# A decoder layer on one core: layernorm of the cross units' tokens moved to where the tokens are made, their rows kept normalized in HBM, and the light parts placed anew

## The chip, the core and the metric

The kernel runs on one core of one Trainium2 chip. The core has five engines with a queue of instructions each: TensorE (PE in the profile; its weight loads are PEld) for matmuls, VectorE (DVE), ScalarE (ACT), GpSimd (POOL), and SyncE (SP), which here only issues DMAs. Each engine works through its queue in order and waits on semaphores for the others. The time is the device time of one execution in microseconds; the figure compared is the median of several executions.

## The reference

Four sequences of 1024 tokens with 512 features, in float32, go through three blocks, each added to its input:

```python
x = x + attn(layernorm(x))            # 16 heads of 32, queries, keys and values from x
x = x + xattn(layernorm(x), ctx_768)  # queries from x, keys and values from a context of 384 features
x = x + ffn(layernorm(x))             # 512 -> 64; 16 relu units for each of the 64; 64 -> 512
```

`layernorm` subtracts the mean over the 512 features and divides by the square root of the variance plus 1e-5. The first attention is gated: the softmax of the scores is multiplied by an aperture for each query and an expression for each key (two sigmoids of `x @ Wa` and `x @ We`) and normalized again; its output is rotated for each head and projected. The second attention is a plain one with biases.

## The kernel before

The work is cut into eight **units**, `order = [(ph, b)]`: units 0 to 3 are the first attention (`ph` 0) of the four sequences, units 4 to 7 the cross attention (`ph` 1) and the feed-forward network. A unit has two **halves** (`hf`) of 512 query tokens. A half's `attention(u, hf)` has 32 **steps**: four groups of four heads (`g`), eight blocks of 128 keys each (`kt`). A step issues the scores (L552), two exponentials on ScalarE (`e`, L557), sums of the exponentials on VectorE (`es`, L563 and L565; in `ph` 0 also the gated sum `eg`, L573), and then the previous step's values times exponentials (`av`, L579) and, in units 0 to 3 and 7 ("shared"), a part of the sums on TensorE (`sm`, L587). When a group is over, `normalize` copies `av`; one step later `add_up` has TensorE add up `es` over the partitions (L609), and the result goes through HBM (`sum_d`, `rec_d`) to `divide` two steps later and `multiply` (L659) two more.

Beside these steps run the **light parts** of other work: `pre(u)` makes a coming unit's inputs (load of tokens, layernorm, transposes, projections `k`, `q` and values `v`, gates), `post(u, hf)` finishes a half (output projection `o` L716, and in `ph` 1 layernorm, network, output). `beside(u, hf)` writes by hand the list of parts that go with a half, and `run` deals them out: each part has a load (2 for two chunks of a projection, 0 for what does no matmul), and after each step parts are issued until their share of the total load matches the share of steps. `weave` spreads the parts of one list evenly among those of another, `pause` is load without work. The queues of TensorE, VectorE, ScalarE and GpSimd have exactly this order; SP's order is made by a scheduler.

A transpose of tokens goes in two moves. `away` writes normalized rows to HBM (`rows_d`, L295) and `back` reads them into another layout with four DMAs (L300); then VectorE transposes blocks of 32 x 32 (`blocks`, L306: four instructions, `tr`). Only the very first tokens are transposed by TensorE (`across`, L313).

What the change touches:

- In `ph` 0, `post` writes the new tokens twice: `x1_d` as they are (L718), and `x1b_d` with the cross attention's output bias added by GpSimd (L720). In `ph` 1, `pre` loads `x1_d` again (L366), takes the statistics (`stats`, L378), their root (`root`, twelve small instructions), normalizes (`norm`, L286), writes the rows and reads them back.
- In `ph` 1, `post` does the same for the feed-forward network: statistics with each `o` (L726), `root` (L731), four `norm`, each into one of two buffers `r2` that a DMA writes to `rows_d`; the last of them also reads back into `xn`. Each `norm` is followed by an addition of `bout_bc` on GpSimd (L747). Then `tr`, `inputs` (L758, which reads `xn`), `hidden` (17 pieces, L773 on ScalarE and L779 on VectorE) and `outputs` (L790, L796).
- `rows_d` lies in three buffers that take turns. The tile `tok` (one buffer) holds both a unit's loaded tokens and `xn`; `inT` (two buffers) holds transposed tokens or context.
- In the prelude, before the first step, `negate` (L142) turns the sign of the gates' bias `nbae`, which eight small DMAs bring.
- While `crossing` is set, that is in all of the eight units, `evacuate` copies on ScalarE, else on VectorE.

Of the kernel before, what the change touches and what calls it, by code (L numbers as in the profile page):

```python
# [16 lines left out]
P = 128  # L17
# [46 lines left out]
def moderate_path(tc: tile.TileContext, a: dict, out: bass.AP, flag: bass.AP):  # L64
    nc = tc.nc
    x = a["x"]
    with ExitStack() as st:
# [26 lines left out]
        x1_d = [[dram.tile([P, D], F32, tag=f"mx1_{b}_{t}", name="x1_d") for t in range(NT)] for b in range(B)]  # L94
# [193 lines left out]
        turns = [0]  # L288

        def away(rows, xt, t, n):  # L290

            if t == 0:
                rows[:] = [dram.tile([4, P, D], F32, tag=f"rows_{turns[0] % 3}", name="rows_d")]
                turns[0] += 1
            nc.sync.dma_start(rows[0][t : t + n].rearrange("t p d -> p t d"), xt)  # L295

        def back(rows, to):

            for q in range(NC):
                nc.sync.dma_start(  # L300
                    to[ts(q, NB)].rearrange("j t (s f) -> j (t s) f", f=P),
                    rows[0].rearrange("t (s j) f -> j (t s) f", j=NB)[:, :, ts(q, P)],
                )
# [36 lines left out]
        def pre(u):  # L340
# [15 lines left out]
            def load_x(hf):  # L356
                def f():
                    if u == 0 and hf == 0:
                        xt = x0
                    else:  # L360
                        xt = p1.tile([P, 4, D], F32, tag="tok", name="xin")
                        if ph == 0:
                            nc.sync.dma_start(xt, x[b].rearrange("(t p) d -> p t d", p=P)[:, 4 * hf : 4 * hf + 4, :])
                        else:
                            for t in range(4):
                                nc.sync.dma_start(xt[:, t, :], x1_d[b][4 * hf + t])  # L366
                    me["xn", hf] = xt
                return f

            def ln(hf):  # L370
# [14 lines left out]
                def norm(t):  # L385
                    def f():
# [4 lines left out]
                        if t % 2:  # L391
                            away(res.setdefault("rows", []), me["xn", hf][:, t - 1 : t + 1, :], t - 1, 2)
                        if t == 3:
                            me["xT", hf] = p2.tile([P, 4, D], F32, tag="inT", name="xT")
                            back(res["rows"], me["xT", hf])
# [131 lines left out]
            for k, f, load in (  # L527
                ("ctx", load_ctx, 0), ("x", load_x, 0), ("g", gates, 1), ("gt", gates_t, 1),
# [154 lines left out]
        def post(u, hf):  # L683
# [18 lines left out]
            def project(t):  # L702
                def part(cs):
                    def f():
# [11 lines left out]
                        nc.vector.tensor_tensor(r, res["po"], r, ALU.add)  # L716
                        if ph == 0:
                            nc.sync.dma_start(x1_d[b][4 * hf + t], r)  # L718
# [3 lines left out]
                        else:  # L722
                            s6 = p2.tile([P, 6], F32, tag="bnst1", name="bnst1")
                            if t == 0:
                                res["mv"] = p2.tile([P, 4, 2], F32, tag="fmv", name="fmv")
                            nc.vector.bn_stats(s6, r)  # L726
                            nc.vector.bn_aggr(res["mv"][:, t, :], s6)
# [3 lines left out]
            def root():  # L731
                i = 2 * NS + b * NT + 4 * hf
                nc.gpsimd.tensor_copy(marks[:, i : i + 4], res["mv"][:, :, 1])
                res["rs"] = rsqrt(res["mv"], 4)
                res["xn"] = p1.tile([P, 4, D], F32, tag="tok", name="xn")

            def norm(t):
                def f():
                    if last:
                        normalized(res["xn"][:, t, :], res[t], res["mv"], res["rs"], t)  # L740
                    else:
                        r2 = p2.tile([P, 1, D], F32, tag="r2", name="r2")
                        normalized(r2[:, 0, :], res[t], res["mv"], res["rs"], t)
                        away(res.setdefault("rows", []), r2, t, 1)
                        if t == 3:
                            back(res["rows"], res["xn"])
                    nc.gpsimd.tensor_tensor(res[t], res[t], bout_bc, ALU.add)  # L747
                return [(0, f)]

# [3 lines left out]
            def inputs():  # L753
# [10 lines left out]
                nc.vector.tensor_copy(sT, ss[:, 0 : 2 * P])  # L764
# [37 lines left out]
            if ph == 0:  # L802
                return {"load": loads, "o": [project(t) for t in range(4)]}
            return {
                "load": loads,
                "o": [project(t) for t in range(4)],
                "ln": [[(0, root)]] + [norm(t) for t in range(4)],
                "tr": [[(1 if last else 0, tr(t))] for t in range(4)],
# [39 lines left out]
        def beside(u, hf):  # L848

            last = post(u, 0) if hf else post(u - 1, 1) if u else None  # L850
            if u + 1 == n:
                out = last["load"] + pause(16) + last["o"] + weave(last["ln"], pause(4)) + pause(4) + last["tr"]
                return out + pause(2) + last["s"] + weave(last["h"], pause(14)) + pause(2) + last["out"]
            p = pres[u + 1]
            x, ln, tr, k, q, v = (p[i] for i in ("x", "ln", "tr", "k", "q", "v"))
            next_ = pres[u + 2] if u + 2 < B else None
            if u + 1 < B:
                if hf == 0:
                    out = x[1] + k[0][0:1] + p["g"][0] + k[0][1:] + p["gt"][0]
                    if last:  # L860
                        out = last["load"] + out + weave(ln[1], last["o"])
# [3 lines left out]
                    return out + v[0][0:2] + tr[1] + v[0][2:3] + p["g"][1] + v[0][3:] + p["gt"][1]  # L865
                if not next_:
                    return k[1] + last["load"] + v[1] + last["o"] + q[0] + q[1]
                out = next_["x"][0] + k[1] + last["load"] + v[1] + last["o"] + weave(next_["ln"][0], q[0])
# [691 lines left out]
```

## Time and profile before

| | |
|---|---|
| median of three runs | 2329.31 us (2329.3 to 2330.63) |
| profiled execution | 2332.95 us, span 2331.2 us |
| mean granted clock of TensorE | 0.983 |
| TensorE busy | 2222.9 us, 95% of the span |
| VectorE, ScalarE, GpSimd busy | 1560.7, 1234.8, 142.5 us |
| HBM read and written | 124.07 and 51.15 MB |

The span is the time from the first to the last instruction of the profiled execution. The profile's slices are 40 equal parts of it, 58.3 us each, with busy tenths (9 is 90% or more); the row PEclk is the granted clock in tenths. A list of waits has the engine and line that waited, what ended the wait, microseconds in total, times, and the longest. A timeline line has the start, the time taken, engine, line, operation, the tile written and the tiles read, the number of instructions run together, and in brackets the idle time ahead and what ended it. The prelude ends and the first step begins at 119.5 us; second halves of units 4, 5 and 6 begin at 1350.3, 1616.0 and 1881.7 us, unit 7 at 2021.0 us.

### The profile page before, as it was taken

To read this page: it belongs to the slowest core of one execution; us is meant where nothing else is said; L and a number is where in the kernel's file an instruction comes from. 1 tells how busy PE (TensorE), PEld (TensorE's weight loads), DVE (VectorE), ACT (ScalarE), POOL (GpSimd) and SP (SyncE) were. 2 spreads that over 40 slices of the span, in tenths; PEclk is the share of its full clock that TensorE was granted. 3 is DMA by queue.
4 is the path that set the end of the run, shared out by engine and by line. 5 is a ranking of instruction groups with operands and counts; after the bars stand their busy time and mean duration, and the time that the engine had idled before them with its cause. 6 is when DMAs were issued, how large, how long until landed. Compare 5 with 4: busy or idle time off the path is not lost.

```text
span 2331.2 us, 52885 instructions
## 1 busy us (share of the span) xinstructions
PE 2222.9 (95%) x22610; PEld 561.3 (24%) x22610; DVE 1560.7 (67%) x2485; ACT 1234.8 (53%) x1478; POOL 142.5 (6%) x146
## 2 busy tenths in 40 slices
PE   5999999999999999999999999999999998999974
PEld 2322222222222222222222222222222222222211
DVE  3368666685677856666865678677976788655544
ACT  0055545555455544555556555657566664756551
POOL 3000011000000000000000001010100101010100
PEclk9999999999999999999999999999999999999996
DMA  4422023130321302102431234222422244211120
GB/s 127 128 78 83 27 85 86 44 125 27 100 81 41 113 30 93 53 24 85 137 95 39 84 97 110 74 65 79 139 54 75 79 137 101 65 40 51 35 59 25
DMA packets 162822, 178.79 MB, mean 77 GB/s; under 512 B 47392, under 2 KB 93088, under 8 KB 161424
## 3 DMA queue, kind: packets, MB, share of 16 engines
q1 hardware_dynamic: 159120, 174.26, 25.2%
q8 instruction: 179, 2.93, 0.5%
q0 software_dynamic: 2144, 0.98, 0.3%
q14 instruction: 67, 0.55, 0.1%
q10 hardware_dynamic: 1312, 0.07, 0.1%
HBM read 124.07 MB, written 51.15 MB: 75 GB/s over the span
## 4 chain that ended last, share of the span: by engine, by line
PE 71%; DVE 12%; DMA 8%; ACT 4%; issue 3%; SPq 1%; ACTq 0%; DVEq 0%; POOL 0%
PE f L87 28%; PE s L552 19%; PE av L579 15%; PE sm L587 5%; DVE es L565 5%; ACT e L557 2%; PE sm L609 2%; DMA xn<-rows_d 2%; DMA rows_d<-r 2%; DMA recb<-rec_d 1%; DMA sum_d<-both 1%; PE f L790 1%; DMA rec_d<-rec 1%; DVE g L779 1%; ACT hid L773 1%
## 5 line engine op out<-in xcount | busy, mean ns | idle before, releaser
L557 ACT ACTIVATE e<-s 128x1024 f32<-128x1024 f32 x1024 | 995.0, 1021 | 758.4 <-PE s L552 568.6
L565 DVE TENSOR_TENSOR es<-es,e 128x1024 f32<-128x1024 f32 x528 | 640.7, 1237 | 262.6 <-ACT e L557 261.8
L552 PE MATMUL s<-q,k 32*64 32x512 f32 x8192 | 636.9, 614 | 11.0 <-ACT e L557 9.5
L579 PE MATMUL av<-e,v 128*32 128x512 f32 x4096 | 559.1, 606 | 0.0
L87 PE MATMUL f<-xT,w 128*32 128x512 f32 x2816 | 334.9, 594 | 0.4 <-PE s L552 0.3
L573 DVE SCALAR_TENSOR_TENSOR eg<-e,sw,eg 128x512 f32<-128x512 f32 x448 | 323.3, 757 | 2.3
L87 PE MATMUL f<-w,q 128*32 128x512 f32 x2048 | 246.3, 598 | 12.1 <-DVE q L659 12.1
L552 PEld LDWEIGHTS s<-q,k 32*64 32x64 f32 x8192 | 140.6, 130 | 475.6 <-ACT e L557 281.3
L563 DVE TENSOR_TENSOR es<-e 128x1024 f32<-128x1024 f32 x88 | 110.0, 1270 | 176.8 <-ACT e L557 168.8
L579 PEld LDWEIGHTS av<-e,v 128*32 128x32 f32 x4096 | 89.4, 108 | 405.3 <-issue 401.4
L87 PEld LDWEIGHTS f<-xT,w 128*32 128x32 f32 x2816 | 95.7, 111 | 212.0 <-issue 201.0
L587 PE MATMUL sm<-e,sw 128*2 128x512 f32 x1024 | 134.2, 596 | 0.0
L773 ACT ACTIVATE hid<-sT,units 128x256 f32<-128x256 f32 x128 | 74.9, 603 | 98.9 <-DVE sT L764 62.0
L720 POOL TENSOR_TENSOR r<-res,bo_bc 128x512 f32<-128x512 f32 x32 | 47.2, 1474 | 1122.8 <-DVE res L716 1018.4
L87 PEld LDWEIGHTS f<-w,q 128*32 128x32 f32 x2048 | 67.2, 111 | 168.9 <-issue 150.1
L87 PE MATMUL f<-w,xT 128*32 128x512 f32 x896 | 105.0, 592 | 0.6 <-DVE q L267 0.6
L87 PE MATMUL f<-w,ctxT 128*32 128x512 f32 x768 | 92.8, 592 | 0.0
L87 PE MATMUL f<-ctxT,w 128*32 128x512 f32 x768 | 92.6, 592 | 0.0
L609 PE MATMUL sm<-es,ones 128*1 128x512 f32 x352 | 74.1, 621 | 17.7 <-DVE es L565 17.0
L779 DVE SCALAR_TENSOR_TENSOR g<-hid,units,g 128x256 f32<-128x256 f32 x120 | 57.9, 482 | 28.6 <-ACT hid L773 20.9
L659 DVE TENSOR_TENSOR q<-both,recb 128x512 f32<-128x512 f32 x64 | 45.3, 708 | 39.0 <-DMA recb<-rec_d 38.8
L716 DVE TENSOR_TENSOR res<-f,res 128x512 f32<-128x512 f32 x64 | 43.8, 685 | 31.2 <-PE f L87 31.1
(238 smaller groups left out, 1067.4 us busy)
## 6 DMA issues: line engine op xcount, KB each, us to landing
recb<-rec_d SPq DMA_DIRECT2D x256, 64.0 KB
rows_d<-xin SPq DMA_DIRECT2D x30, 512.0 KB
xT<-rows_d SPq DMA_DIRECT2D x60, 256.0 KB
w<-in_xattn_Wo SPq DMA_DIRECT2D x9, 1024.0 KB
xin<-in_x SPq DMA_DIRECT2D x8, 1024.0 KB
res<-in_x SPq DMA_DIRECT2D x32, 256.0 KB
w<-wout_d SPq DMA_DIRECT2D x8, 1024.0 KB
x_d<-res SPq DMA_DIRECT2D x32, 256.0 KB
```

The costliest lines, as they stand in the source:

```text
L87: nc.tensor.matmul(to[r], lhsT=lhsT[:, j, :] if len(lhsT.shape) == 3 else lhsT[:, r], rhs=rhs, **flags)
L552: nc.tensor.matmul(s[m : m + 64, j, :], lhsT=k[r, g, kt * P + m : kt * P + m + 64], rhs=q[r, g, :], start=True, stop=True,)
L557: nc.scalar.activation(e, s, AF.Exp, scale=SCALE)
L563: nc.vector.tensor_tensor(me["es"][i], me["e", 0][i], es[i], ALU.add)
L565: nc.vector.tensor_tensor(me["es"][i], me["es"][i], es[i], ALU.add)
L573: nc.vector.scalar_tensor_tensor(eg, es[0][:, h, :], gate(kt), eg, ALU.mult, ALU.add)
L579: nc.tensor.matmul(av[r, :], lhsT=me["v"][:, kt, HG * g + h, :], rhs=es[h // 2][:, h % 2, :], start=(kt == 0), stop=(kt == NT - 1),)
L587: nc.tensor.matmul(sm[j * DH : j * DH + sums, :], lhsT=me["sw"][:, t, HG * g + 2 + h, :] if ph == 0 else ones, rhs=me["e", t][1][:, h, :], ...
L609: nc.tensor.matmul(sm[j * DH : j * DH + 1, :], lhsT=ones, rhs=e, start=True, stop=True)
L720: nc.gpsimd.tensor_tensor(r2, r, bo_bc, ALU.add)
L773: nc.scalar.activation(hid, res["s"], AF.Relu, bias=units[:, 1, h : h + 1], scale=units[:, 0, h : h + 1])
L779: nc.vector.scalar_tensor_tensor(res["g"], res["hid"], units[:, 2, h - 1 : h], res["g"], ALU.mult, ALU.add)
```

## The change

The statistics, root and normalization of the tokens that the cross attention reads move from `pre` of units 4 to 7 to `post` of units 0 to 3; the tokens are no longer written to HBM as they are, only normalized (`rows_d`, now a buffer for each half of each sequence). Reading back is a part of its own (`xT`), as is the addition of the network's output bias (`b`). The negation stands behind the first keys. `sT` is copied by `evacuate`. The lists in `beside` are written anew; among others the first two values of a unit's second half go to the first half.

```diff
-        x1_d = [[dram.tile([P, D], F32, tag=f"mx1_{b}_{t}", name="x1_d") for t in range(NT)] for b in range(B)]
+        rows_d = [[dram.tile([4, P, D], F32, tag=f"rows_{b}_{i}", name="rows_d") for i in range(2)] for b in range(B)]
...
 def load_x(hf): ...
-                        if ph == 0:
-                            nc.sync.dma_start(xt, x[b].rearrange("(t p) d -> p t d", p=P)[:, 4 * hf : 4 * hf + 4, :])
-                        else:
-                            for t in range(4):
-                                nc.sync.dma_start(xt[:, t, :], x1_d[b][4 * hf + t])
+                        nc.sync.dma_start(xt, x[b].rearrange("(t p) d -> p t d", p=P)[:, 4 * hf : 4 * hf + 4, :])
+            def load_xT(hf):
+                def f():
+                    me["xT", hf] = p2.tile([P, 4, D], F32, tag="inT", name="xT")
+                    back(rows_d[b][hf], me["xT", hf])
+                return f
...
 post: def project(t): ...
                         nc.vector.tensor_tensor(r, res["po"], r, ALU.add)
+                        s6 = p2.tile([P, 6], F32, tag="bnst1", name="bnst1")
+                        if t == 0:
+                            res["mv"] = p2.tile([P, 4, 2], F32, tag="fmv", name="fmv")
+                        nc.vector.bn_stats(s6, r)
+                        nc.vector.bn_aggr(res["mv"][:, t, :], s6)
                         if ph == 0:
-                            nc.sync.dma_start(x1_d[b][4 * hf + t], r)
...
+            def load_xT():
+                res["xn"] = p1.tile([P, 4, D], F32, tag="tok", name="xn")
+                back(rows_d[b][hf], res["xn"])
+            def biased(t):
+                return lambda: nc.gpsimd.tensor_tensor(res[t], res[t], bout_bc, ALU.add)
...
-                nc.vector.tensor_copy(sT, ss[:, 0 : 2 * P])
+                evacuate(sT, ss[:, 0 : 2 * P])
...
 beside(u, hf): last = post(u, 0) if hf else post(u - 1, 1)
   unit 7:
-                out = last["load"] + pause(16) + last["o"] + weave(last["ln"], pause(4)) + pause(4) + last["tr"]
-                return out + pause(2) + last["s"] + weave(last["h"], pause(14)) + pause(2) + last["out"]
+                out = last["load"] + pause(16) + last["o"] + weave(last["ln"], pause(4)) + last["xT"] + pause(4)
+                out += last["tr"] + weave(last["b"], pause(4)) + last["s"] + weave(last["h"], pause(12))
+                return out + pause(2) + last["out"]
   next unit in ph 0, first half:
-                        out = last["load"] + out + weave(ln[1], last["o"])
+                        out += weave(ln[1], last["o"]) + xT[1] + weave(last["ln"], v[0][0:2])
   next unit in ph 0, second half:
-                out = next_["x"][0] + k[1] + last["load"] + v[1] + last["o"] + weave(next_["ln"][0], q[0])
-                out += q[1][0:3] + next_["tr"][0] + q[1][3:]
+                out = next_["x"][0] + k[1][0:2] + last["load"] + weave(next_["ln"][0], k[1][2:] + v[1]) + last["o"]
+                out += weave(last["ln"], q[0][0:2]) + q[0][2:] + next_["xT"][0] + q[1][0:3] + next_["tr"][0] + q[1][3:]
   next unit in ph 1, first half (with a network to do):
-                out += k[0][0:3] + v[0][0:1] + last["o"] + weave(last["ln"], v[0][1:2]) + v[0][2:3] + last["tr"]
-                return out + v[0][3:] + last["s"] + weave(last["h"], k[1]) + k[0][3:] + last["out"]
+                out += k[0][0:3] + v[0][0:1] + last["o"] + weave(last["ln"], v[0][1:3]) + last["xT"] + v[0][3:]
+                out += last["b"][0:2] + k[1][0:1] + last["tr"] + k[0][3:] + last["b"][2:] + last["s"]
+                return out + weave(last["h"], k[1][1:] + v[1][0:1]) + v[1][1:2] + last["out"]
   next unit in ph 1, second half (units 3 to 6; the network in 4 to 6):
-            out = x[0] + last["load"] + v[1][0:1] + weave(ln[0], v[1][1:3]) + v[1][3:] + x[1] + last["o"][0:1] + tr[0]
-            out += weave(ln[1], last["o"][1:])
-            out += weave(last["ln"], q[0][0:1]) + q[0][1:2] + tr[1] + last["tr"] + q[0][2:3] + last["s"]
-            return out + weave(last["h"], q[0][3:] + q[1][0:3]) + q[1][3:] + last["out"]
+            out = xT[0] + last["load"] + v[1][2:] + tr[0] + xT[1] + q[0][0:2] + last["o"][0:2] + tr[1] + last["o"][2:]
+            out += weave(last["ln"], q[0][2:3])
+            out += last["xT"] + last["b"][0:2] + q[0][3:] + last["tr"] + q[1][0:1] + last["b"][2:] + last["s"]
+            return out + weave(last["h"], q[1][1:]) + last["out"]
   prelude:
-        first = p["x"][0] + p["ln"][0] + one(negate) + p["tr"][0] + p["k"][0] + p["x"][1] + p["g"][0]
+        first = p["x"][0] + p["ln"][0] + p["tr"][0] + p["k"][0] + p["x"][1] + one(negate) + p["g"][0]
```

## The prediction

> **What bounds the kernel now.** I read first the page's busy times and slices, then the list of what TensorE waited for, then timelines around its longest waits, then the order in which the two programs' instructions stand.
>
> ```profile
> PE 2222.9 (95%) x22610; PEld 561.3 (24%) x22610; DVE 1560.7 (67%) x2485; ACT 1234.8 (53%) x1478; POOL 142.5 (6%) x146
> PE   5999999999999999999999999999999998999974
> PEclk9999999999999999999999999999999999999996
> DMA  4422023130321302102431234222422244211120
> ```
>
> TensorE is the bound, and the change gives it the same matmuls. So only its idle time counts: 2331.2 - 2222.9 = 108 us, and the time it works at a lower clock. No DMA slice is half full, so the 16.8 MB that the change no longer moves (32 tiles of 256 KB written and read) buy nothing by themselves. The waits (us in total, times, longest):
>
> ```profile
> PE sm L609 <- DVE es L565: 17.0, 7, 5.3
> PE f L758 <- DVE xn L306: 15.0, 9, 5.2
> PE f L313 <- DVE xin L286: 12.9, 1, 12.9
> PE f L313 <- DVE xin L267: 11.8, 1, 11.8
> ```
>
> The third, and the waits of the program's end (12.1, 10.9 and 4.8 us in the same list), stay as they are. The others are touched.
>
> **Start: the negation.** In the timeline VectorE stands at `nbae` until the last bias has landed, ahead of the copies that free the banks for TensorE's block transposes:
>
> ```profile
> 27.55 0.15 DVE L142 TENSOR_SCALAR nbae<-nbae 128x1 f32<-128x1 f32 x1 [13.33 <-DMA nbae<-in_attn_be]
> 28.40 3.64 PE L313 MATMUL f<-ident,xin 128*32 128x128 f32 x64 [11.81 <-DVE xin L267]
> 32.85 13.94 PE L87 MATMUL f<-xin,w 128*32 128x512 f32 x128 [0.81 <-DVE xin L267]
> ```
>
> After, `negate` stands behind the key copies. The second transposes can start at 16.6 + 0.7 (a copy), end at 21, and the keys are ready to go at 21.9. Next late is their weight: it comes in four parts, issued at 6.8, 7.8, 10.5 and 14.4; the third lands at 20.85 in the chain. The fourth holds the completion lane for which SP's third part of the query weight waits until 26.16, so I put it there. Three quarters of the first key group run before; the group ends at 27.0 and the keys at 27.0 + 3 x 3.43 = 37.3, where before they ended at 46.8: -9.5. The queries then start at 38.2; their weight's last part is issued by 28.9, and at the keys' 10.4 us lands at 39.3: about a microsecond of waiting, half of it felt. Term: **-9** (-12 if the fourth part lands with the third, -5 if the query weight is four later).
>
> **Second halves of units 4 to 6: the wait for the sums.** The timeline of TensorE at the first of them, and VectorE's line inside:
>
> ```profile
> 1418.21 1.11 PE L552 MATMUL s<-q,k 32*64 32x512 f32 x16
> 1424.28 1.87 PE L609 MATMUL sm<-es,ones 128*1 128x512 f32 x4 [4.96 <-DVE es L565]
> 1430.86 1.11 PE L552 MATMUL s<-q,k 32*64 32x512 f32 x16
> 1434.62 1.11 PE L552 MATMUL s<-q,k 32*64 32x512 f32 x16
> ```
>
> ```profile
> 1422.34 0.76 DVE L286 TENSOR_SCALAR r<-res,fmv,yi 128x512 f32<-128x512 f32 x1 [1.87 <-DMA rows_d<-r]
> ```
>
> This is step 17 of 32. `add_up` needs the sum of step 15, and VectorE has been held up by the next unit's layernorm (woven among `o`), then by `root` at step 13 and four `norm` at step 14, one waiting for its buffer. Score to score takes 12.65 us here against 3.76 and 0.86 for the sums: 8.0 lost, not 5.0, because the matmuls after it are slow: the granted clock of 1424.3 to 1431.1 is 0.71. The same lines in units 5 and 6 give 8.6 and 8.8. After, the order of instructions has no next-unit layernorm here, and `root` at the end of step 15, behind the sum that `add_up` wants, the other `norm` at step 17: **-25.4** (-20 to -27). The buffer wait of about 3 us stays, but is next needed at step 25.
>
> **Unit 7 and first halves of 5 and 6: the wait for the transposed rows.**
>
> ```profile
> 2100.27 2.49 DVE L306 STREAM_TRANSPOSE xn<-xn 128x512 f32<-128x512 f32 x4 [5.31 <-DMA xn<-rows_d]
> ```
>
> ```profile
> 2101.63 4.81 PE L758 MATMUL f<-xn,win 128*32 128x256 f32 x32 [5.22 <-DVE xn L306]
> ```
>
> In unit 7 `tr` keeps its step (19), but `inputs` goes from step 21 to 22. One step without a part is 1.1 + 1.1 + 1.0 = 3.2 us, so 2.0 of the 5.2 stay, and with a short gap (1.5 us at 1566.7 leaves the clock at 1.00) the slow spell after it (clock 0.57 over 6.8 us, here 2 to 3 us) goes: -5.5 in each half, **-11** (-15 to -4). In units 5 and 6 the gaps of 1.5 + 0.6 and 1.2 + 0.6 go, since `inputs` has a step more: **-3.5**. Unit 3's second half loses a wait of 0.9: **-1**.
>
> **The price: queries right behind their transposes.** In the second halves `xT[0] ... tr[0] + xT[1] + q[0]` puts at the end of step 3 the four transposes, and in the same step in units 4 to 6 the first matmuls that read them. Before, seven steps lay between. VectorE's queue holds the two additions of step 3 ahead of them, and these wait for the exponentials. What a step looks like now:
>
> ```profile
> 1643.54 1.11 PE L552 MATMUL s<-q,k 32*64 32x512 f32 x16
> 1644.69 1.95 ACT L557 ACTIVATE e<-s 128x1024 f32<-128x1024 f32 x2 [2.04 <-PE s L552]
> 1645.46 1.90 PE L87 MATMUL f<-w,q 128*32 128x512 f32 x16
> ```
>
> Exponentials end at 1646.6, the second addition (1.2) at 1647.9 to 1648.2, four transposes (2.5) at 1650.4 to 1650.7; TensorE is ready at 1645.46. It would wait 4.9 to 5.2 us, just as at the sums, and by that row (8.0 with the slow clock) the price is 3 x 8.0 = **+24** (+15 without slow clock; +31 if small divides ahead of the additions add 2). Queued behind it are all of TensorE's scores. Unit 3 has scores and values of step 4 between: 1.2 to 1.5, **+1.5**.
>
> The Trainium skill, "TensorE: Matmul & The Clock Gate" ("Part 1: The HAM clock gate"), says that the clock halves after one idle window of some 3.4 us, in windows that run freely. This trace agrees at 5 us of idling (0.71) and at 1.5 us (1.00); a rule read strictly would spare a 5.2 us gap that straddles two windows, and with every one spared the sum would be 9 us lower.
>
> **Smaller ones.** `hidden` is pressed into 6 steps instead of 8: ACT then has 6 x 2.04 + 16 x 0.6 + 2.4 = 24.3 us against TensorE's 23.5, 1 us more in each of some four halves, with `sT`'s copy moved to ACT: **+4** (0 to +8). Units 1 and 2 gain on VectorE in their first halves 4 x 0.87 (statistics) + 2.4 (`root`) + 2.0 (`norm`) = 7.9 us. At step 23 some 3.6 us of lag are left over the idle time, and the sums of step 25 have 3.1 us of slack in the trace: **+1** (0 to +4). SP's issues: four writes of `x1_d` per half become four of `rows_d`, reads are fewer, and `load_xT` stands later than the writes that it reads, so SP blocks less. POOL's adds move to steps 18 to 22 and are used at 30: nothing. The reads of `rows_d` in units 4 to 7 are of rows written some 900 us earlier: nothing.
>
> **Sum.** -9 - 25.4 - 11 - 3.5 - 1 + 24 + 1.5 + 4 + 1 = -19.4. The profiled execution took 2332.95 us (span 2331.2) and would take 2313.5; it lies 3.6 above the median of 2329.31, so I predict 2310. Its own range, from the ends of the terms taken together, is 2298 to 2322.
>
> **Rivals.** (1) *The queries do not wait.* If TensorE comes to step 3 as late as VectorE, +24 falls away: 2286. For it: TensorE is in places held by ACT (9.5 us of waits on `e`). Against: the row above shows 5 us of lead. (2) *The new wait is longer.* If the transposes themselves wait for `xT<-rows_d` (such a read takes 6.3 us in the chain), 3 x 6 comes on top: 2328, no change. Against: SP has it ahead of the previous half's outputs. (3) *Slower: layernorm in phase 0 makes VectorE the bound.* In first halves VectorE is already busy 46.35 of 55 us (735 to 790). If its lag passes the 3.1 us of slack by 5, each sum of steps 17 and 25 in units 1 and 2 costs the 8 us seen at step 17: 4 x 8 = +32, so 2342. Against: its idle time ahead of step 23 is 4.5 us, and the second halves have more.
>
> **Numbers.** Forecast 0.62, rival 1 0.18, rival 2 0.12, rival 3 0.08. Differences of over 0.2% (4.7 us) can be told from none: faster 0.79, same 0.12, slower 0.09. The range reaches down to rival 1 and up to near rival 2: 2285 to 2326.
>
> **What would show it.** Right: keys at about 22 with a gap before their fourth chunk; no wait of 5 us at the sums; three new waits of `f` on `xT` of about 5 us, each with a slow spell; `f` on `xn` down to 1 to 2 us. Wrong: no wait on `xT`, sums still waiting at step 17, or new waits on `es` or `eg` in units 1 and 2.

## The result: no change that can be measured, and the profile after

The changed kernel took 2329.94 us in the median of twelve runs (2323.08 to 2332.77), beside 2330.05 us (2327.65 to 2333.62) for the kernel before on the same chip: a ratio of 0.9996, with an interval of 0.9987 to 1.0004. Two repetitions, told below, gave 0.9994 and 0.9991. The forecast was 2310 us.

The profiled execution after is the quickest of its twelve, 2323.08 us with a span of 2321.1; that of before, 2332.95, lay 2.9 above its median. So the two traces differ by 10.1 us of span where the medians differ by 0.1. The traces show what moved; how much of their 10 us is luck comes at the end.

Lines shift by about five: scores are L547 (L552 before), exponentials L552, additions L558 and L560, `add_up` L604, `multiply` L654, block transposes L302. From the page of after, the busy times and the slices of TensorE, its clock and the DMAs:

```profile
PE 2214.6 (95%) x22610; PEld 556.3 (24%) x22610; DVE 1556.0 (67%) x2478; ACT 1237.3 (53%) x1485; POOL 136.9 (6%) x146
...
PE   6999999999999999999999999998999989999984
...
PEclk9999999999999999999999999999999999999997
DMA  4422032041311312112222212231222332102020
```

TensorE is the bound as before. Busy time fell by 8 us with the same matmuls, although 57 us of it now lie in spells of half clock where 44 did; busy time also holds short waits (experiment 9), and what made it shorter isn't shown in full. Its list of waits (us in total, times, longest):

```profile
PE s L547 <- ACT e L552: 22.6, 24, 3.5
PE f L87 <- DVE xT L302: 15.9, 4, 4.9
...
PE f L790 <- DVE res L796: 8.8, 3, 4.0
...
PE f L758 <- DVE xn L302: 2.1, 4, 0.6
```

The 17.0 us at the sums are gone and the 15.0 at `inputs` are 2.1, as forecast. The second line is the forecast's new wait on `xT`, three times 4.92 us and once 1.13. The first (9.5 before) and the third (0.8 before) are more than it had.

**As forecast: the sums.** TensorE at step 17 of unit 4's second half, in the timeline:

```profile
1412.22 1.11 PE L547 MATMUL s<-q,k 32*64 32x512 f32 x16
1413.27 1.04 PE L604 MATMUL sm<-es,ones 128*1 128x512 f32 x8
...
1416.81 1.11 PE L547 MATMUL s<-q,k 32*64 32x512 f32 x16
```

From the scores of one step to those of the next takes 4.6 us, where it took 12.6; in units 5 and 6 it was 13.2 and 13.4 and is 4.6 as well.

**As forecast: the queries behind their transposes.** Step 3 of the same half, VectorE, then TensorE:

```profile
1354.95 2.36 DVE L560 TENSOR_TENSOR es<-es,e 128x1024 f32<-128x1024 f32 x2 [1.89 <-ACT e L552]
1357.23 2.48 DVE L302 STREAM_TRANSPOSE xT<-xT 128x512 f32<-128x512 f32 x4
```

```profile
1359.77 2.79 PE L87 MATMUL f<-xT,w 128*32 128x512 f32 x12 [4.92 <-DVE xT L302]
```

The two additions wait for the exponentials, the transposes stand behind them, TensorE waits 4.92 us. The three steps 3 take 10.4, 10.3 and 10.6 us, where they took 4.0 before.

**Not forecast: the outputs of units 5 and 6's first halves.** At step 31 TensorE waits 4.00 us (3.95 in unit 6) for a bank, because VectorE has not yet added the first outputs (`res`, L796). VectorE stands still before that, at `multiply`, and SP's queue shows why:

```profile
1600.64 0.69 DVE L654 TENSOR_TENSOR q<-both,recb 128x512 f32<-128x512 f32 x1 [6.34 <-DMA recb<-rec_d]
1601.25 4.62 DVE L560 TENSOR_TENSOR es<-es,e 128x1024 f32<-128x1024 f32 x4
1605.79 1.28 DVE L796 TENSOR_TENSOR res<-f,res 128x512 f32<-128x512 f32 x2
```

```profile
1583.55 3.02 SPq L92 DMA_DIRECT2D w<-in_xattn_Wq  x4
1587.96 0.34 SPq L644 DMA_DIRECT2D rec_d<-rec  x1
1597.02 1.73 SPq L648 DMA_DIRECT2D recb<-rec_d  x4
```

The reciprocals are written out at 1587.96 and may be read back only when the write has landed: 9.1 us later, where the round before took 1.45 (1555.51 to 1556.96). Ahead of the 8 KB stand the 1024 KB of the next unit's query weight. It takes the buffer that the key weight leaves. In the new lists the keys end ahead of the last values, so the buffer is free earlier, and the scheduler of SP's queue put the read in front; before, it stood behind the reciprocals' rows.

**Mis-sized: the hidden units.** Steps 23 to 25 of unit 5's second half, on ACT and on VectorE:

```profile
1706.53 1.94 ACT L552 ACTIVATE e<-s 128x1024 f32<-128x1024 f32 x2 [0.65 <-PE s L547]
1708.35 1.09 ACT L773 ACTIVATE hid<-sT,units 128x256 f32<-128x256 f32 x2
1713.14 0.60 ACT L773 ACTIVATE hid<-sT,units 128x256 f32<-128x256 f32 x1 [3.70 <-DVE g L777]
1713.64 1.92 ACT L552 ACTIVATE e<-s 128x1024 f32<-128x1024 f32 x2
```

```profile
1705.89 6.89 DVE L560 TENSOR_TENSOR es<-es,e 128x1024 f32<-128x1024 f32 x6
1712.70 0.40 DVE L777 TENSOR_SCALAR g<-hid,units,fb 128x256 f32<-128x256 f32 x1
```

`hid`, the tile of a hidden unit, has two buffers. Two hidden units fill them; the third has to wait until VectorE has read the first, and VectorE has six additions to do ahead of that. ACT stands for 3.70 us, and the exponentials that TensorE wants are queued behind. TensorE waits 3.46 us (2.32 and 2.56 in units 4 and 6), and then its clock halves. Two stretches of that, in units 4 and 5: after the stretch's length come the busy times of TensorE, its weight loads, VectorE, ScalarE and GpSimd, then the granted clock, the DMAs' share and GB/s:

```profile
1443.00:1450.00 7.00, 6.21 (x44) 1.33 (x48) 2.88 (x5) 6.00 (x9) 0.00 (x0) 0.76 0.01 2
1714.00:1721.00 7.00, 6.30 (x36) 1.41 (x40) 2.75 (x5) 6.02 (x9) 0.00 (x0) 0.54 0.01 2
```

### The profile page after: what moved, and what is told of

Its sections match the earlier page's. It is cut to its first block, busy times and chain, and to the rows that moved or that the text cites. A ratio compares the mean times of both kernels' runs of the same rounds, so it can differ in the third digit from the quotient of the medians.

```text
span 2321.1 us, 52855 instructions
## 1 busy us (share of the span) xinstructions
PE 2214.6 (95%) x22610; PEld 556.3 (24%) x22610; DVE 1556.0 (67%) x2478; ACT 1237.3 (53%) x1485; POOL 136.9 (6%) x146
## 3 DMA queue, kind: packets, MB, share of 16 engines
q1 hardware_dynamic: 150160, 157.48, 22.6%
## 4 chain that ended last, share of the span: by engine, by line
PE 82%; DVE 5%; DMA 5%; ACT 4%; issue 3%; SPq 1%; DVEq 0%; ACTq 0%
PE f L87 33%; PE s L547 22%; PE av L574 18%; PE sm L582 5%; PE sm L604 3%; ACT e L552 2%; DVE es L560 2%; DMA rec_d<-rec 2%; ACT hid L773 1%; PE f L790 1%; DMA w<-in_attn_Wo 1%; DVE g L779 1%; DMA recb<-rec_d 1%; DMA rows_d<-r 1%; SPq L648 0%
## 5 line engine op out<-in xcount | busy, mean ns | idle before, releaser
L552 ACT ACTIVATE e<-s 128x1024 f32<-128x1024 f32 x1024 | 994.3, 1021 | 767.3 <-PE s L547 579.3
L560 DVE TENSOR_TENSOR es<-es,e 128x1024 f32<-128x1024 f32 x528 | 637.7, 1233 | 265.1 <-ACT e L552 263.9
L547 PE MATMUL s<-q,k 32*64 32x512 f32 x8192 | 635.0, 616 | 24.8 <-ACT e L552 22.6
L568 DVE SCALAR_TENSOR_TENSOR eg<-e,sw,eg 128x512 f32<-128x512 f32 x448 | 318.4, 746 | 2.3
L547 PEld LDWEIGHTS s<-q,k 32*64 32x64 f32 x8192 | 138.5, 130 | 490.4 <-ACT e L552 288.3
L558 DVE TENSOR_TENSOR es<-e 128x1024 f32<-128x1024 f32 x88 | 110.3, 1276 | 205.2 <-ACT e L552 184.0
L719 POOL TENSOR_TENSOR r<-res,bo_bc 128x512 f32<-128x512 f32 x32 | 40.9, 1277 | 1111.5 <-DVE res L711 1056.5
L604 PE MATMUL sm<-es,ones 128*1 128x512 f32 x352 | 68.5, 621 | 0.7 <-ACT both L593 0.7
L654 DVE TENSOR_TENSOR q<-both,recb 128x512 f32<-128x512 f32 x64 | 45.0, 703 | 34.5 <-DMA recb<-rec_d 34.1
L287 DVE TENSOR_SCALAR r<-res,fmv,yi 128x512 f32<-128x512 f32 x60 | 37.1, 635 | 38.4 <-DMA rows_d<-r 37.8
```

What stands on the lines that cost most here:

```text
L547: nc.tensor.matmul(s[m : m + 64, j, :], lhsT=k[r, g, kt * P + m : kt * P + m + 64], rhs=q[r, g, :], start=True, stop=True,)
L552: nc.scalar.activation(e, s, AF.Exp, scale=SCALE)
L558: nc.vector.tensor_tensor(me["es"][i], me["e", 0][i], es[i], ALU.add)
L560: nc.vector.tensor_tensor(me["es"][i], me["es"][i], es[i], ALU.add)
L568: nc.vector.scalar_tensor_tensor(eg, es[0][:, h, :], gate(kt), eg, ALU.mult, ALU.add)
L604: nc.tensor.matmul(sm[j * DH : j * DH + 1, :], lhsT=ones, rhs=e, start=True, stop=True)
```

## The experiments

Sixteen runs followed, each in five rounds beside the kernel before. Where the changed kernel ran on the same chip, differences are against that; otherwise against 0.9994 of before.

**1. The changed kernel again, twice** (second time beside experiments 11 to 13).

> The changed kernel, unchanged. Theory T (the forecast gains came, and three new waits ate them: queries behind their transposes 3 x 6 to 8 us, the query weight ahead of the reciprocals' rows 2 x 4 to 6 us, hidden units with two buffers 10 to 15 us in all): within 0.2% of before, and this profile shows the same waits again: three of about 4.9 us on xT at step 3 of the second halves of units 4 to 6, two of about 4 us at the outputs of the first halves of units 5 and 6, waits on e of about 22 us in all. Rival S (the waits differ from execution to execution, and the profiled one, 7 us under its own median, was a lucky one): the waits stand in other places or are over 8 us larger in sum.

> The changed kernel, unchanged, beside the three that follow on the same chip: within 0.2% of before, profile within 4 us of its median, waits as in the earlier profiles.

Measured: 2325.9 us against 2326.86, ratio 0.9994 [0.9986, 1.0003]; 2327.97 against 2330.44, 0.9991 [0.9980, 1.0002]. The waits stood in the same places with the same sizes: 4.92 us three times on `xT`, 3.5 and 3.4, then 3.7 and 3.75 at the outputs, 22.0 and 22.3 on `e`. So a theory of lucky executions doesn't hold for the three waits.

**2. The negation alone, in the kernel before.**

```diff
-        first = p["x"][0] + p["ln"][0] + one(negate) + p["tr"][0] + p["k"][0] + p["x"][1] + p["g"][0]
+        first = p["x"][0] + p["ln"][0] + p["tr"][0] + p["k"][0] + p["x"][1] + one(negate) + p["g"][0]
```

> The kernel before with the negation alone moved behind the keys. Theory T: the forecast's start term holds, -9 us (-5 to -12), and the prelude up to the first scores is 5 to 9 us shorter than its 119.5. Rival S (what the start gains is given back at the fourth part of the weight or in the first unit): -2 to +1. Rival C (TensorE's granted clock gives back whatever idle time is taken away): under -3, with a lower mean clock than before's 0.983.

Measured: 2318.72 us, -8.1; ratio 0.9969 [0.9958, 0.9980], prelude 113.7 in place of 119.5, mean clock 0.984. The forecast's term holds, and with it the gap that it put ahead of the fourth chunk:

```profile
20.07 2.78 PE L87 MATMUL f<-xin,w 128*32 128x512 f32 x24 [0.81 <-DVE xin L267]
26.15 14.26 PE L87 MATMUL f<-xin,w 128*32 128x512 f32 x104 [3.31 <-DMA w<-in_attn_Wo]
```

**3. The transposes early, in the changed kernel.**

```diff
-            out = xT[0] + last["load"] + v[1][2:] + tr[0] + xT[1] + q[0][0:2] + last["o"][0:2] + tr[1] + last["o"][2:]
+            out = xT[0] + tr[0] + last["load"] + v[1][2:] + xT[1] + q[0][0:2] + last["o"][0:2] + tr[1] + last["o"][2:]
```

> The changed kernel with the first four block transposes of the next unit at step 0 of the second halves of units 3 to 6 instead of right ahead of the queries. Theory T: the three waits of 4.9 us and the slow matmuls behind them go, step 3 falls from 10.4 to about 4 us: -18 to -24 against the changed kernel, -1 of it in unit 3. Rival C (the granted clock gives it back): -3 to -8. Rival V (VectorE is so late there that the wait moves on to the sums or to the next copies): -5 to -10, with new waits on es or res in steps 4 to 9.

Measured: 2305.08 us, -20.8; ratio 0.9910 [0.9896, 0.9923]. Step 3 takes 3.8 us in all three units. The price of the new wait is what theory T says, and little of it comes back elsewhere: beside the profile of experiment 1 the three second halves are together 20.1 us shorter, the first halves of units 5 and 6 0.8 longer each.

**4. The keys last, in the changed kernel.**

```diff
-                return out + weave(last["h"], k[1][1:] + v[1][0:1]) + v[1][1:2] + last["out"]
+                return out + weave(last["h"], v[1][0:2] + k[1][1:3]) + k[1][3:] + last["out"]
```

> The changed kernel with the values ahead of the keys in the last part of the first halves of units 5 and 6, so that the key weight's buffer, which the query weight takes, comes free after the reciprocals' rows are on their way. Theory T: the reciprocals' rows land about 6 us earlier, VectorE's stall of 6.3 us at the product and TensorE's of 4.0 us at the outputs go: -8 to -13 against the changed kernel. Rival H (the stall comes from ACT's hidden units, not from the weight): 0 to -3, with the 4.0 us at the outputs still there.

Measured: 2318.34 us, -7.6, just short of theory T's 8 to 13; ratio 0.9964 [0.9951, 0.9977]. The order of SP's queue changed as meant, the waits at the outputs fell to 0.8 us in all, and the first halves of units 5 and 6 are 5.1 and 3.6 us shorter. A part went elsewhere: the weight now stands among the outputs' traffic, the next sums come back late to VectorE, which has the transposes behind them.

```profile
1625.36 0.25 DVE L641 RECIPROCAL rec<-cs 128x16 f32<-128x16 f32 x1 [4.04 <-DMA cs<-sum_d]
...
1628.00 2.48 DVE L302 STREAM_TRANSPOSE xT<-xT 128x512 f32<-128x512 f32 x4
```

```profile
1630.54 3.64 PE L87 MATMUL f<-xT,w 128*32 128x512 f32 x16 [7.06 <-DVE xT L302]
```

**5. Both together.**

> The changed kernel with the early transposes and the keys last together. Theory T: the waits are apart and the two add up: at least -28 against the changed kernel (-21 and -8 alone), and more, about -34, because the transposes at step 0 no longer wait behind the query weight (alone, the keys last made the waits on xT 7.1 and 8.1 us in place of 4.9). Rival V (VectorE's lag only moves on): -21 to -25.

Measured: 2290.66 us against 2329.57, ratio 0.9832 [0.9819, 0.9846], so -38 against the changed kernel, more than 20.8 and 7.6. With the transposes early, the wait that experiment 4 moved has nothing to hold up, and by the ratios of experiments 3 and 5 the weight's place is then worth some 18 us.

**6. Three buffers for the hidden units, in the changed kernel.** The gates' exponentials of units 0 to 3 share them.

```diff
-                    gi = p2.tile([P, P], F32, tag="gi", name="gi")
+                    gi = p2.tile([P, 2 * P], F32, tag="hid", name="gi", bufs=3)[:, 0:P]
...
-                        hid = p2.tile([P, 2 * P], F32, tag="hid", name="hid")
+                        hid = p2.tile([P, 2 * P], F32, tag="hid", name="hid", bufs=3)
```

> The changed kernel with three buffers in place of two for the hidden units' tile (the gates' exponentials of phase 0 share them, to fit the memory). Theory B (ACT stands at the third hidden unit of a step until VectorE, behind with its additions, has read the first; the next exponentials are queued behind it): TensorE's waits on e fall from about 22 to 10 us and the half-speed spells of the second halves of units 4 to 6 go: -6 to -12 against the changed kernel. Rival A (ACT simply has more work in these six steps than TensorE): 0 to -2, waits on e still about 20 us.

Measured: 2302.14 us, ratio 0.9882 [0.9867, 0.9897]: -26, over twice what theory B said. The waits on `e` fell from 22.6 to 7.3 us, and step 25 of the second halves from 7.1, 8.3 and 8.8 to 5.5. ACT does the same work, so its sum is not the cause.

**7. All three together.**

> The changed kernel with the early transposes, the keys last and three buffers for the hidden units. Theory T: all three prices gone, so what the forecast took away (about -50 in the profile, with -5 for what stays of ACT) is seen: 2280 to 2290, -36 to -46 against the changed kernel. Rival A (three buffers do not help): as the two edits without them.

Measured: 2266.35 us, ratio 0.9725 [0.9711, 0.9739], -63 against before and -62 against the changed kernel: 16 to 26 more than theory T had.

```profile
PE f L309 <- DVE xin L287: 12.9, 1, 12.9
PE f L87 <- DVE q L654: 11.8, 1, 11.8
PE f L790 <- DVE g L779: 10.6, 1, 10.6
PE s L547 <- ACT e L552: 6.0, 15, 1.9
```

What TensorE waits for now, above all, is the program's start (the first line) and its end (the next two).

**8. Only the finished half's layernorm two parts later, in the kernel before.**

```diff
-            out += weave(last["ln"], q[0][0:1]) + q[0][1:2] + tr[1] + last["tr"] + q[0][2:3] + last["s"]
-            return out + weave(last["h"], q[0][3:] + q[1][0:3]) + q[1][3:] + last["out"]
+            out += q[0][0:1] + weave(last["ln"], q[0][1:2]) + tr[1] + q[0][2:3] + last["tr"] + q[0][3:] + last["s"]
+            return out + weave(last["h"], q[1]) + last["out"]
```

> The kernel before with only the layernorm of the finished half put two parts later in the second halves of units 4 to 6 (and its transposes, inputs and hidden units behind it), so that VectorE adds up the exponentials first; the next unit's layernorm stays woven among the output projection, and the rows are stored and read as before. Theory P (the place of root and norm makes the sums wait): the three waits of 5 us at the sums of step 17 go with their slow spells: -20 to -25 against the kernel before, less up to 8 for new waits at inputs. Rival L (the next unit's layernorm holds VectorE up, and only its removal helps): 0 to -8, with the sums still waiting 3 to 5 us.

Measured: 2322.1 us, -7.5; ratio 0.9968 [0.9957, 0.9980]. Step 17 takes 4.6 us in all three units, with the next unit's layernorm still beside it: the place of `root` and `norm` made the sums wait (theory P), not the work that the change takes out of these halves. The rest went into a new wait at `inputs`, whose step takes 10.0 to 10.2 us in place of 3.8:

```profile
PE f L758 <- DVE xn L306: 23.9, 10, 4.8
```

**9. Three buffers in the kernel before** (the edit of experiment 6).

> The kernel before with three buffers in place of two for the hidden units' tile. Theory N (the price of two buffers is new: with two hidden units in a step ACT waits for VectorE, but TensorE does not feel it): 0 to -6, so that some 20 of the 27 us that three buffers gave the changed kernel are the change's own loss. Rival O (the kernel before paid it too): -12 to -25, and the change itself lost little by it.

Measured: 2304.43 us, -21.3; ratio 0.9910 [0.9895, 0.9925]. Theory N falls: the kernel before paid for its two buffers as well. TensorE's list of waits shows only 5 us of it,

```profile
PE s L552 <- ACT e L557: 4.1, 9, 2.0
```

where 9.5 us in 20 waits stood before. Most of it hides in TensorE's busy time, which is 2202.4 us where it was 2222.9. Two steps of the kernel before, both at full clock, show how:

```profile
2090.51 2.00 PE L552 MATMUL s<-q,k 32*64 32x512 f32 x16
...
2094.30 1.11 PE L552 MATMUL s<-q,k 32*64 32x512 f32 x16
```

A step's 16 matmuls of scores take 1.11 us when nothing holds them. When the second eight wait for ScalarE's exponentials, the group takes up to 2.00, and all of it counts as busy. Added up over the steps at full clock, the time beyond 1.11 us is 64 us in the kernel before and 47 with three buffers. By the difference of the two experiments, only some 5 of the 26 us of experiment 6 are new with the change.

**10. The forecast's term alone, in the kernel before.**

```diff
-            return out + weave(last["h"], q[0][3:] + q[1][0:3]) + q[1][3:] + last["out"]
+            return out + q[0][3:] + weave(last["h"], q[1][0:3]) + q[1][3:] + last["out"]
...
-                nc.vector.tensor_copy(sT, ss[:, 0 : 2 * P])
+                evacuate(sT, ss[:, 0 : 2 * P])
```

and the pauses of unit 7, 14 to 12.

> The kernel before with one term of the forecast alone: the hidden units of the second halves of units 4 to 6 woven into six parts in place of eight, with unit 7's pauses cut from 14 to 12, and sT copied by ACT. The forecast's term for it was +4 (0 to +8), from ACT's sum of work. Theory B (two buffers couple ACT to VectorE's lag): +10 to +18, with waits on e of about 20 us in place of 9.5. Rival A (only the sum of work counts): 0 to +8.

Measured: 2328.85 us against 2325.69, +3.2; ratio 1.0012 [1.0002, 1.0023]. So pressing into six parts, by itself and in the kernel before, costs about what the forecast said; theory B's 10 to 18 did not come. That it costs more where VectorE is behind is what experiment 12 bears on.

**11. SP's order alone: the context's read behind the reciprocals' rows.**

```diff
-            out += last["xT"] + last["b"][0:2] + q[0][3:] + last["tr"] + q[1][0:1] + last["b"][2:] + last["s"]
+            out += last["xT"] + last["b"][0:2] + q[1][0:1] + last["tr"] + q[0][3:] + last["b"][2:] + last["s"]
```

> The changed kernel with the last group of the first half's queries and the first group of the second half's exchanged, which changes nothing in the order of VectorE, but lets SP issue the next unit's context read (1.5 MB in two, it takes a buffer that these queries free) behind the reciprocals' rows in place of ahead of them, in units 4 and 5. Theory Q (a big read that an earlier freed buffer lets start stands between the reciprocals' write and their read back; the product comes late on VectorE, the additions behind it, and so ACT's third hidden unit): VectorE's wait of 2.1 us at the product in unit 5 goes and the scores' wait of 3.5 us at step 25 there falls under 2: -3 to -6 against the changed kernel, none of it in unit 6. Rival A (the hidden units' place alone makes the stall): 0 to -1.

Measured: 2328.53 us, +0.6 against the changed kernel; ratio 0.9991 [0.9982, 1.0000]. Theory Q falls, at least for the context. The reciprocals' write still takes 5.6 us, now with only the finished half's rows (four reads of 256 KB issued from 1700.01) ahead of it:

```profile
1700.01 1.93 SPq L296 DMA_DIRECT2D xn<-rows_d  x4
1701.98 0.49 SPq L644 DMA_DIRECT2D rec_d<-rec  x1
1707.57 1.71 SPq L648 DMA_DIRECT2D recb<-rec_d  x4
1709.37 1.36 SPq L344 DMA_DIRECT2D ctxT<-in_ctxT  x1
```

**12. ACT's order alone: two hidden units first, in the changed kernel.**

```diff
-            return out + weave(last["h"], q[1][1:]) + last["out"]
+            parts = sum(q[1][1:], [])
+            return out + last["h"][0:2] + [parts[0:1]] + weave(last["h"][2:], [parts[1:]]) + last["out"]
```

> The changed kernel with two hidden units in place of three ahead of the first part that follows the inputs, in the second halves of units 4 to 6; all others one part later, three to a part as before. Theory F (the third hidden unit of the first part finds both buffers taken while VectorE has six additions ahead of the first accumulation; the next exponentials wait behind it on ACT): the waits of 2.3, 3.5 and 2.6 us at step 25 and the slow spells behind them go: -8 to -14 against the changed kernel. Rival A (three to a part is too much for ACT wherever it starts): 0 to -3, with waits on e still about 22 us.

Measured: 2316.83 us, -11.1; ratio 0.9939 [0.9926, 0.9953]. Steps 24 and 25 of unit 5's second half took 5.6 and 8.3 us and take 2.2 and 5.5; the waits on `e` are

```profile
PE s L547 <- ACT e L552: 14.5, 23, 1.9
```

The other hidden units still come three to a part. So neither six parts nor ACT's work costs these 11 us, but the one place where three hidden units with two buffers meet VectorE's six additions (theory F).

**13. The four edits together** (3, 4, 6 and 11).

> The kernel of early transposes, keys last and three buffers, with the context read later as well. Theory Q: little is left of that wait with three buffers: 0 to -3 against those three, so 2262 to 2267 where before stands at 2329. Rival: slower by 2 to 6 us, if the next unit's transposes now wait for the context's place.

Measured: 2264.16 us against 2330.44, ratio 0.9720 [0.9707, 0.9733]; the same as three.

**14. The query weight cut by rows of partitions, in the changed kernel,** and **15. all quartered weights so, on top of experiment 13.**

```diff
-                dma(to[:, c, :], w.rearrange("(q c i) f -> c q i f", c=NC, i=NB)[c])
+                dma(to[ts(c, NB), :, :], w.rearrange("(q c i) f -> q i c f", c=NC, i=NB)[c])
```

> The changed kernel with the cross units' query weight read in the same four DMAs of 256 KB and at the same place, but each cut by 32 rows of partitions with all chunks in place of one chunk over all partitions. In the trace the read runs at 103 GB/s on a fifth of the DMA engines for 10 us, and the 8 KB of reciprocals issued 4.4 us behind it land 9.1 us after their issue. Theory W (few engines carry this read, and the reciprocals queue on the same ones): cut by 32 rows it takes 3 to 5 us, the reciprocals land 4 to 6 us earlier, the 4.0 us at the outputs of the first halves of units 5 and 6 fall under 1: -6 to -12 against the changed kernel, with no instruction of an engine moved. Rival H (VectorE is late there for another reason, or the read is bound by HBM): 0 to -2.

> The best kernel so far (early transposes, keys last, three buffers, later context) with all weights that are read in quarters cut by 32 rows in place of chunks. Theory W: the prelude's waits for weights (3.3 to 3.9 us at the keys) go, and what the first weights block behind them: -3 to -8 against 2264 (before at 2330). Rival (a first chunk must now wait for all four parts, where it waited for one): 0 to +5.

Measured for 14: 2313.69 us against 2324.45, ratio 0.9945 [0.9927, 0.9963], against the changed kernel -9 by the medians and -11 by the ratios; the first halves of units 5 and 6 take 130.8 us in place of 134.1 and 134.2, and the waits at the outputs there are gone. While the weight comes in, the changed kernel and this one show (the DMAs' share and GB/s are the last two numbers):

```profile
1586.00:1596.00 10.00, 8.76 (x88) 2.13 (x84) 6.92 (x12) 7.10 (x11) 0.00 (x0) 1.00 0.27 103
```

```profile
1591.00:1592.00 1.00, 1.00 (x16) 0.37 (x16) 0.90 (x3) 0.06 (x1) 0.00 (x0) 1.00 0.74 234
```

A quarter of the DMA engines' time went into the read before (not the fifth of the expectation), three quarters do now. But the scheduler, too, set SP's order anew: one of the four parts ahead of the reciprocals' write, one between write and read, two behind. So the run doesn't tell the cut from the place, and which of them makes how much of the gain stays open. Measured for 15: 2256.39 us, ratio 0.9701 [0.9685, 0.9717], by the ratios some 4 us less than experiment 13. The keys still wait 3.7 us for their weight, but ahead of the first chunk, and the prelude takes 111.7 us. It is the quickest version of all, 68 us ahead of the kernel before and 67 ahead of the changed one.

## Why the prediction was wrong

The forecast's sum beside the two traces, in us. Steps are taken from the start of one step's scores to that of the next; units as a whole, since the change moves two values (some 5 us of matmuls) from second to first halves.

| term | forecast | traces |
|---|---|---|
| start, unit 0 (to 404.8, then to 393.1) | -9 | -11.7 |
| units 1 and 2 | +1 | -0.1 |
| unit 3 | +0.5 | -1.7 |
| sums, step 17 | -25.4 | -25.5 |
| `inputs` in units 5 and 6, first halves (7.5, 7.2 to 4.7, 4.8) | -3.5 | -5.2 |
| queries, step 3 (3.8 without the wait; 10.4, 10.3, 10.6) | +24 | +19.9 |
| outputs, step 31 of the first halves of 5 and 6 (3.6 to 8.7) | 0 | +10.2 |
| the step after it (3.8 to 5.2 and 5.6) | 0 | +3.3 |
| hidden units, and the rest of units 4 to 6 (+12.1 in all) | +3 | +9.4 |
| unit 7 with its hidden units, and the end | -10 | -8.6 |
| sum (the spans differ by 10.1, the executions by 9.9) | -19.4 | -10.0 |

**Right.** The start: -8.1 alone. The sums: the removal to a tenth of a microsecond, and its reason, `root` and `norm` behind the sum, by experiment 8. The new wait: 4.92 us for "4.9 to 5.2", where it was put, -20.8 when taken away. A slow spell came with each of the three, so none of the 9 us came that the prediction allowed for spared gaps; a wait cost 6.6 a time, not 8.0, since the slow matmuls behind it (clock 0.50 from about 1359.6 to 1363) added 1.7 us to the wait, where they had added 3 at the first of the sums. In unit 7 0.6 us of each wait at `inputs` stayed, where the forecast left 2.0. Rival 1 (no wait) and rival 3 (VectorE the bound in units 1 and 2: 560.8 us from the end of unit 0 to the start of unit 3, where it was 560.9) did not come. Rival 2 named nearly the time, 2328, but by luck: its mechanism is wrong, since the transposes did not wait for their rows.

**Wrong, first: a term that is missing.** The smaller terms said of SP's queue that it "blocks less" and gave it nothing. They counted the rows that the change writes and reads, and not the weights, whose place in SP's queue hangs on when another weight's last matmul frees the buffer. The lists' new order of keys and values moved that, and 1024 KB came to stand ahead of 8 KB on which VectorE's queue hung: +13.5 in the table, 7.6 to 18 by experiments 4 and 5.

**Wrong, second: a term mis-sized.** `hidden` was costed by ACT's sum of work, +4 (0 to +8), of which +3 lie in units 4 to 6. The table has +9.4 there, together with what else changed in these units, and 8.6 of it stand in steps 24 to 28 of the second halves; experiments 6 and 9 put what is new at some 5. So the size lies between 5 and 9.4. (The 11.1 us that go when the first three hidden units are split are more than the change's own loss: steps 24 and 25 of unit 5 then take 7.7 us together, where the kernel before took 10.2.) What was left out is the buffer: with two, ACT is tied to VectorE's lag, and VectorE's lag there is six additions, in unit 5 because the transposes (1.4 us) and `multiply` (2.1 us) had just waited for DMAs. The forecast looked at each queue, and not at the tile that joins them.

**Wrong, third: the time from the trace.** The forecast took the 3.6 us by which the trace of before lay above its median off the result, as if the trace of after would lie above its own by as much. Beside the twelve times of the result, the trace of before lay 2.9 above the median and that of after 6.9 below. Part of the latter is the start. With the negation out of the way the next thing is the second half's rows, at 67 to 73 us, and that wait is not the same in each execution: TensorE's gap there is 0.6 us in the trace of after, and 0.7 to 6.0 in ten other profiles whose start is in the same order. In the worst, that of experiment 12,

```profile
73.01 3.64 PE L87 MATMUL f<-xT,w 128*32 128x512 f32 x16 [5.99 <-DVE xT L302]
```

the matmuls behind it run at half clock (16 in 3.64 us, for 1.90), and the prelude takes 119.3 us, as before the change; in the others it takes 112.8 to 116.6. Prelude and unit 0 together end at 395.6 us in the mean of eleven such profiles, against 403.7 of four with the old start: -8, not -11.7. That is 2.5 of luck in the trace of after, so the 9.9 us between the two executions become 7.4, and 4.5 with the 2.9 of before; the three ratios give 0.9 to 2.1. What the remaining 2.4 to 3.6 us are is open.

## What to carry to other kernels

Before costing a reordered list, write down for each big read which buffer it takes and which instruction frees that buffer: the read moves with that instruction, and a small round trip through HBM that an in-order engine waits for is what it hits. Where two engines share a tile with two buffers, cost a denser stretch by how far the reader is behind at its first piece, not by the writer's sum of work; an extra buffer is a cheap test, and here it was worth 21 us in a kernel whose list showed only 9.5 us of such waits. And take a trace's luck into account before forecasting from its microseconds: one execution is one draw.

## What the runs showed of the hardware

A wait need not be as long as five microseconds to halve the clock. In the changed kernel gaps of 2.32, 3.46 and 2.56 us on TensorE were each followed by a granted clock of 0.50, for about 3.4, 6.8 and 6.8 us (from 1445, 1714.5 and 1987.6), while a gap of 1.90 us at 119.0 left it at 1.00. The length of the gap alone does not decide: gaps of 1.85 us in the kernel before (124.8, which the prediction did not look at) and 1.97 us in the changed kernel's third profile (118.5) were followed by such a spell too, and one of 2.49 us in experiment 4 (1985.2) was not. The spell can begin when TensorE is at work again. By an estimate, the gap and half of the spell, the wait of 2.56 us cost some 6. The Trainium skill, "TensorE: Matmul & The Clock Gate" ("Part 1: The HAM clock gate"), gives one idle window of some 3.4 us, free-running, as what halves the clock. Spells of one or two times 3.4 us agree with such windows; the gaps of 2.3 and 2.6 us, shorter than a window, do not fit "idle for a whole window", and the measurement decides.

The read of a quartered weight used 0.25 to 0.27 of the DMA engines' time and ran at 103 GB/s with little else under way, and an 8 KB write issued 4.4 us behind it landed 9.0 us after its issue, when the rate had dropped to 23 GB/s (1596 to 1597). The Trainium skill, "DMA: Bandwidth & Descriptors" ("Why a DMA increments its semaphore by 16 and not by 1"), says that a DMA is split over the largest number of engines, up to 16, that divides the slowest dimension of both sides, and that on a hardware queue (as the profile lists this one, `hardware_dynamic`) these are the lowest-numbered ones; which engines were used, no run here shows. The slowest dimension of that read is 4, and 4 of 16 engines agree with the share; cut by 32 rows, 256 KB had a share of 0.74 at 234 GB/s in the one microsecond shown.
